# Two attention layers on one core: entry 0's scores in four column strips, the projections of the later entries spread over all of entry 0's pass, and the seams between entries rearranged

## The chip, the core and the metric

The kernel runs on one core of a Trainium2 chip. It is written with a tile framework that places buffers and semaphores; TensorE's instructions run in the order in which the program writes them, those of the other engines in the order that the framework's planner makes from the program order and its own estimates of readiness. The metric is the device time of one execution in microseconds. Engines: PE (TensorE, matrix products; PEld its weight loads), DVE (VectorE), ACT (ScalarE), POOL (GpSimd) and SP (SyncE, which issues most of the DMAs).

## The reference

A batch of 8 entries x[2048, 256] goes through two graph attention layers over the same adjacency matrix adj[2048, 2048], each followed by a residual and a layer norm.

```
layer 0 (8 heads of 32):  x_proj = x W_h;  e_src = x_proj a_src,  e_dst = x_proj a_dst
    e[i,j] = leaky_relu(e_src[i] + e_dst[j], 0.2) + softplus(beta) log(adj[i,j] + 1e-6),  no edge: masked
    h[i]   = sum_j softmax_j(e) x_proj[j]       (per head);   x1 = layernorm(x + h W_out^T)
layer 1:  e = leaky_relu((x1 W1)(x1 W2)^T, 0.2), no edge: masked
    h'[i]  = sum_j softmax_j(e) (x1 W3)[j];     out = layernorm(x1 + relu(h'))
```

## The kernel before

**Layer 0** (class `Gat`, one per entry) never forms the exponent of each pair. The exponent of a leaky ReLU of a sum is the larger of two products, so a tile of 128 keys by 2048 queries is `max(c, r) * mt` in one DVE operation (L336): `c` the query factors of a head, spread over all partitions, `r` a per-key number (`re`), `mt` the mask column, which also holds the adjacency to the power beta. The second per-key factor is multiplied into the value rows `v` beforehand (`scale`, L286). A *unit* is one block of 128 keys for two heads: two L336 tiles, then on PE one product with the values into `val` and one with the per-key factor into `den` (`products`, L361; 16 records each, in four groups of 32 columns). An entry has 64 units: 4 pairs of heads (`hp`) by 16 key blocks (`jt`). For some key blocks (`SUMMED`, L67) DVE or ACT adds the scaled tile to a running sum instead (L343, L349), and PE takes den from the sum at the end. `finish` (L373 to L389) divides: den goes through DRAM and a reciprocal, and one multiply (L389) scales two pairs of heads. There are 4 buffers for score tiles `s`, 2 for `mt`, 3 for `c`.

`output` (L391) applies W_out (L414), adds x, which it loads itself in four pieces `xg` (L400), and takes the layer norm, in four steps. `turn` (L430) transposes x1 (L439) and forms h3 = x1 W3 (L445), in eight steps. **Layer 1** (class `Dot`) has 16 steps of 128 query rows: scores `e` (L475) one step ahead, masked row minimum on DVE (L480), exponent (L481), transposes `pt` (L494) and the product `acc` with h3 (L510).

**The order around the change.** At the start, `scores_first` (L246) computes e_dst and e_src of entry 0 for all 16 row blocks, in 32 products with 128 rows of x as weights and only 16 moving columns; `factors` (L268) then takes their maximum over all rows (one GpSimd reduction) and forms the exponents. In the *first stage* entry 0's 64 units run alone; between them `others()` (L539) computes the projections of the seven other entries, an item for each quarter of an entry: transposes of x (L172), rows (L262), and after the fourth quarter factors, scaling and the store of `v` and `re` to DRAM. The main loop (L575) asks for an item after every second unit, so that the 28 items are done at the 56th unit. Entry 1 comes last, since its values stay in SBUF. The value buffers are two: `v`, and the one that is later h3; the items use them in turns. The first 16 units also build `mt` from the adjacency (L180 to L193).

After that, entry b's layer 0 runs beside entry b-1's layer 1: the loop from L584 mixes `dot.step(fill)`, where `fill(0)`, `fill(1)` and `fill(2)` put units ahead of the step's transposes, before and after `acc`. A *seam* is the stretch in which layer 0 of an entry has ended and its `output` and `turn` are put between the last layer 1 steps of the entry before and the first units of the next one. There `load` (L300) fetches `v` and `re` of the next entry from DRAM. SP issues these loads, the `xg` of `output`, the mask columns, masks and residual rows in one queue: an issue that waits for its buffer holds up those behind it.

Of the kernel before, what the change touches and what calls it, by code (L numbers as in the profile page):

```python
# [9 lines left out]
F32 = mybir.dt.float32  # L10
# [8 lines left out]
P = 128  # L19
# [8 lines left out]
def kernel(  # L28
# [26 lines left out]
    nc = tc.nc  # L55
    B, N, D = x.shape
    H, _, DH = w_proj.shape
    NT = N // P
    KC = D // P
    BK = 512  # L60
    NB = N // BK
    HALF = N // 2
    HP = 2
    NP = H // HP
    IG = BK // P
# [3 lines left out]
    const = ctx.enter_context(tc.tile_pool(name="const", bufs=1))  # L69
# [3 lines left out]
    chunk = ctx.enter_context(tc.tile_pool(name="chunk", bufs=2))  # L73
    small = ctx.enter_context(tc.tile_pool(name="small", bufs=3))
# [3 lines left out]
    def mm_tile(name):  # L78
        return ps.tile([P, BK], F32, tag="mm", name=name)
# [9 lines left out]
    ident = const.tile([P, P], F32)  # L89
# [15 lines left out]
    beta_c = beta[:, 3:4]  # L105


    wp = const.tile([P, KC, D + 2 * H], F32)
    for kc in range(KC):
        nc.sync.dma_start(  # L110
            wp[:, kc, 0:D].rearrange("p (h f) -> p h f", h=H),
            w_proj[:, kc * P:(kc + 1) * P, :].rearrange("h p f -> p h f"),
        )
    for a, dst in ((a_dst, wp[:, :, D:D + H]), (a_src, wp[:, :, D + H:])):
        a_bc = small.tile([P, D], F32, tag="row", name="a_bc", bufs=4)
        nc.sync.dma_start(a_bc, bass.AP(tensor=a.tensor, offset=a.offset, ap=[[0, P], [1, D]]))
        for kc in range(KC):
            wa = small.tile([P, D], F32, tag="row", name="wa", bufs=4)
            nc.vector.tensor_mul(wa, wp[:, kc, 0:D], a_bc)
            nc.vector.tensor_reduce(dst[:, kc, :], wa.rearrange("p (h f) -> p h f", h=H), AX.X, ALU.add)  # L120
# [36 lines left out]
    v_d = dram.tile([B, P, NT, D], F32, name="v_d")  # L157
    re_d = dram.tile([B, P, 2, NT, H], F32, name="re_d")
# [73 lines left out]
    class Gat:  # L232
# [12 lines left out]

        def scores_first(self, xt):  # L246

            t = mm_tile("both")
            for it in range(NT):
                for kc in range(KC):  # L250
                    nc.tensor.matmul(t[:, ts(it, 2 * H)], xt[:, kc, ts(it, P)], wp[:, kc, D:],
                                     start=(kc == 0), stop=(kc == KC - 1))
            nc.scalar.copy(self.both.rearrange("p t h -> p (t h)"), t[:, 0:NT * 2 * H])

        def rows(self, g, xt, scores=True):

# [11 lines left out]
        def factors(self):  # L268

            top = small.tile([P, 2, H], F32, name="top", bufs=1)  # L270
            ed, es = self.both[:, :, 0:H], self.both[:, :, H:2 * H]
            nc.vector.tensor_reduce(top[:, 0, :], ed.rearrange("p t h -> p h t"), AX.X, ALU.max)
            nc.gpsimd.partition_all_reduce(top[:, 1, :], top[:, 0, :], P, bass_isa.ReduceOp.max)
            self.sums_c = small.tile([P, H, NT], F32, name="cs", bufs=1)
            nc.vector.tensor_tensor(self.sums_c, es.rearrange("p t h -> p h t"),
                                    top[:, 1, :].unsqueeze(2).to_broadcast([P, H, NT]), ALU.add)
            nc.vector.tensor_tensor(ed, ed, top[:, 1:2, :].to_broadcast([P, NT, H]), ALU.subtract)
            self.re = small.tile([P, 2, NT, H], F32, name="re", bufs=2)
            nc.scalar.activation(self.re[:, 0], ed, AF.Exp, scale=-(1.0 - ALPHA))
            nc.scalar.activation(self.re[:, 1], ed, AF.Exp)  # L280

# [17 lines left out]

        def load(self):  # L300
            self.v = whole.tile([P, NT, D], F32, name="v")
            nc.sync.dma_start(self.v, v_d[self.b])
            self.re = small.tile([P, 2, NT, H], F32, name="re", bufs=2)
            nc.sync.dma_start(self.re, re_d[self.b])

        def query_rows(self, h):

# [83 lines left out]
        def output(self):  # L391


            b = self.b
            xb = x[b].rearrange("(t p) d -> p t d", p=P)
            xs = []

            def load(g):
                xs.append(chunk.tile([P, IG, D], F32, tag="ht", name="xg", bufs=3))
                nc.sync.dma_start(xs[g], xb[:, ts(g, IG), :])  # L400

            for g in range(NB - 1):
                load(g)
            for g in range(NB):
                if g == 1:
                    load(NB - 1)
                st = small.tile([P, IG, nc.vector.BN_STATS_DIM], F32, name="st4", bufs=1)
                mv = small.tile([P, IG, nc.vector.BN_AGGR_DIM], F32, name="mv4", bufs=2)
                z = self.ht[:, ts(g, IG)].rearrange("p t k i -> p t (k i)")
                for k in range(0, IG, 2):  # L410
                    y = mm_tile("y").rearrange("p (t c) -> p t c", t=2)
                    for i in range(2):
                        for kc in range(KC):
                            nc.tensor.matmul(y[:, i, :], self.ht[:, g * IG + k + i, kc, :], wot[:, kc, :],  # L414
                                             start=(kc == 0), stop=(kc == KC - 1))
                    nc.vector.tensor_add(z[:, k:k + 2, :], y, xs[g][:, k:k + 2, :])
                    for i in range(k, k + 2):
                        nc.vector.bn_stats(st[:, i, :], z[:, i, :])
                        nc.vector.bn_aggr(mv[:, i, :], st[:, i, :])
                f = small.tile([P, 2, IG], F32, name="f4", bufs=2)  # L420
                nc.scalar.activation(f[:, 0, :], mv[:, :, 1], AF.Ln, bias=eps_ln)
                nc.scalar.activation(f[:, 0, :], f[:, 0, :], AF.Exp, scale=-0.5)
                nc.vector.scalar_tensor_tensor(f[:, 1, :], mv[:, :, 0], -1.0, f[:, 0, :], ALU.mult, ALU.mult)
                for k in range(IG):
                    nc.scalar.activation(z[:, k, :], z[:, k, :], AF.Identity, bias=f[:, 1, k:k + 1],
                                         scale=f[:, 0, k:k + 1])
                nc.scalar.dma_start(x1_d[b].rearrange("(t p) d -> p t d", p=P)[:, ts(g, IG), :], z)
                yield
# [94 lines left out]
    gats = [Gat(b) for b in range(B)]  # L523
# [15 lines left out]
    def others():  # L539


        items = [(gat, g) for gat in gats[2:] + gats[1:2] for g in range(NB)]
        xgs, xts = [], []

        def load(n):
            if n < len(items):
                xgs.append(load_x(items[n][0].b, items[n][1]))

        def turn(n):
            if n < len(items):  # L550
                xts.append(chunk.tile([P, KC, BK], F32, tag="ht", name="xt", bufs=3))
                transpose_x(xgs[n], xts[n])
                load(n + 1)

        load(0)
        turn(0)
        for n, (gat, g) in enumerate(items):
            turn(n + 1)
            if g == 0:
                gat.begin(("v", "h3")[n // NB % 2])  # L560
            gat.rows(g, xts[n])
            if g == 0 and n > 0:
                items[n - 1][0].queries()
            if g == NB - 1:
                gat.factors()
                for k in range(NB):
                    gat.scale(k)
                if gat.b > 1:
                    gat.store()
            yield  # L570
        gats[1].queries()
        yield

    pieces = [others(), later_weights()]
    for k in range(NP * NT):  # L575
        g0.step()
        if k % 2 == 1:
            next(pieces[0], None)
            if k > NT and k % 4 == 1:
                next(pieces[1], None)  # L580


    dot = None
    for b in range(1, B + 1):  # L584
        gat, fresh = gats[b - 1], gats[b] if b < B else None

        def layer_0(count):
            if fresh:
                fresh.step(count)

        if b > 1 and fresh:
            fresh.load()
        rows = gat.output()

        def output(count):
            for _ in range(count):
                next(rows)

        if dot is None:
            layer_0(3)  # L600
            output(4)
            layer_0(1)
        else:

            dot.step(lambda k: layer_0((0, 0, 2)[k]))
            dot.step(lambda k: (output((1, 1, 2)[k]), layer_0((0, 1, 1)[k])))
        for _ in gat.turn():
            layer_0(1)
        dot = Dot(gat)
        dot.step(lambda k: layer_0((2, 1, 1)[k]))  # L610
        for i in range(NT - 3):
            dot.step(lambda k: layer_0((0, 2 - (i % 3 == 2), 2)[k]))
    dot.step()
# [32 lines left out]
```

## Time and profile before

4389.39 us, median of 3 runs (4389.17 to 4393.52). The profiled execution spans 4389.8 us.

| engine | busy us | share | what most of it is |
|---|---|---|---|
| PE | 4243.0 | 97% | val and den products (L361), acc (L510), e (L475) |
| DVE | 3624.5 | 83% | score tiles (L336: 2353.5), sums (L343: 632.2) |
| ACT | 1666.5 | 38% | exponents and copies out of PSUM |
| POOL | 6.4 | 0% | eight reductions of the factors |

The DMA engines are busy 54.6% of the span. Busy PE is modelled from pipelined records, so it is an upper limit. The page divides the span into forty slices of 110 us and gives busy shares in tenths; the table by stage gives the same for any stretch. Entry 0's layer 0 ends at about 488 us; from then on an entry takes about 508.5 us (from one load of `v` to the next), and the last stage, from about 4050 us, is layer 1 of the last entry alone.

### The profile page before, as it was taken

The numbers are of one execution on the slowest core, as the hardware profiler recorded it, in microseconds if no ns is written. First come the engines' busy times: TensorE is split into PE (matmuls) and PEld (weight loads), VectorE is DVE, ScalarE is ACT, GpSimd is POOL, SyncE is SP. The second block draws the span as 40 slices with busy tenths as digits, with TensorE's granted clock in tenths as the row PEclk, the third lists the DMA queues.
The fourth block names the chain that finished last, engine by engine and source line by source line (L and its number), as shares of the span: only waits on it lengthen the run. The fifth ranks groups of instructions, "written<-read, shape, count | busy, mean of one in ns | idle before, by whom it ended". The sixth has DMA issues, their size and how long they took to land.

```text
span 4389.8 us, 59761 instructions
## 1 busy us (share of the span) xinstructions
PE 4243.0 (97%) x25052; PEld 2226.0 (51%) x25052; DVE 3624.5 (83%) x2597; ACT 1666.5 (38%) x3020; POOL 6.4 (0%) x14
## 2 busy tenths in 40 slices
PE   7899899999999999999999999999999999999999
PEld 5454344445444545445445454445555454545666
DVE  6888888998989898997989988898889889898222
ACT  6622233333333323333333334333333333333454
POOL 0000000000000000000000000000000000000000
PEclk9999999999999999999999999999999999999999
DMA  7887666656555554556555555556545565554111
GB/s 234 292 302 273 209 221 211 230 193 225 191 189 189 197 197 168 195 192 213 180 193 185 188 196 185 192 187 216 184 166 199 184 214 184 191 183 147 60 50 41
DMA packets 250958, 839.10 MB, mean 191 GB/s; under 512 B 32320, under 2 KB 150848, under 8 KB 175424
## 3 DMA queue, kind: packets, MB, share of 16 engines
q1 hardware_dynamic: 215360, 801.71, 52.1%
q10 hardware_dynamic: 35328, 33.56, 2.2%
q8 instruction: 196, 3.21, 0.3%
q14 instruction: 74, 0.61, 0.0%
HBM read 761.53 MB, written 73.14 MB: 190 GB/s over the span
## 4 chain that ended last, share of the span: by engine, by line
PE 56%; DVE 18%; issue 9%; DMA 4%; ACT 2%; SPq 1%; ACTq 0%; DVEq 0%
PE acc L510 15%; PE e L475 14%; DVE s L336 11%; PE val L361 11%; PE den L361 7%; DVE d L343 4%; PE pt L494 4%; DMA mt<-mt_d 3%; PE y L414 2%; PE h1p L465 2%; PE h3p L445 1%; DVE p L480 1%; ACT p L481 1%; DMA rc<-dn 1%; SPq L379 0%
## 5 line engine op out<-in xcount | busy, mean ns | idle before, releaser
L336 DVE SCALAR_TENSOR_TENSOR s<-c,re,mt 128x2048 f32<-128x2048 f32 x1024 | 2353.5, 2342 | 194.4 <-PE den L361 132.8
L361 PE MATMUL val<-s,v 128*32 128x512 f32 x8192 | 1030.0, 604 | 67.8 <-DVE s L336 67.3
L510 PE MATMUL acc<-h,pts 128*128 128x256 f32 x4096 | 949.9, 380 | 2.2 <-ACT pts L496 1.4
L475 PE MATMUL e<-x1t,h 128*128 128x512 f32 x2048 | 906.0, 595 | 6.8 <-ACT h L467 6.8
L510 PEld LDWEIGHTS acc<-h,pts 128*128 128x128 f32 x4096 | 748.1, 190 | 92.8 <-ACT pts L496 6.9
L361 PE MATMUL den<-s,re 128*32 128x512 f32 x5568 | 709.0, 599 | 3.3 <-ACT dn L376 3.3
L343 DVE SCALAR_TENSOR_TENSOR d<-s,re,d 128x2048 f32<-128x2048 f32 x272 | 632.2, 2344 | 0.0
L475 PEld LDWEIGHTS e<-x1t,h 128*128 128x128 f32 x2048 | 379.1, 190 | 459.5 <-issue 416.5
L496 ACT COPY pts<-pt 128x512 f32<-128x512 f32 x512 | 298.2, 583 | 766.4 <-PE pt L494 759.5
L361 PEld LDWEIGHTS val<-s,v 128*32 128x32 f32 x8192 | 244.3, 110 | 676.4 <-issue 516.3
L477 ACT ACTIVATE p<-e 128x512 f32<-128x512 f32 x512 | 303.1, 596 | 433.6 <-PE e L475 429.9
L480 DVE CUSTOM_DVE_ANT_0 p<-p,pen 128x2048 f32<-128x2048 f32 x128 | 292.9, 2288 | 198.2 <-ACT p L477 197.5
L361 PEld LDWEIGHTS den<-s,re 128*32 128x32 f32 x5568 | 194.3, 111 | 429.6 <-issue 417.0
L494 PEld LDWEIGHTS pt<-ident,p 128*128 128x128 f32 x2048 | 239.0, 141 | 223.2 <-issue 163.0
L481 ACT ACTIVATE p<-p,neg 128x2048 f32<-128x2048 f32 x128 | 256.7, 2006 | 242.4 <-DVE neg L480 242.4
L494 PE MATMUL pt<-ident,p 128*128 128x128 f32 x2048 | 319.3, 279 | 6.5 <-ACT p L481 6.5
L517 ACT ACTIVATE z<-acc,rec 128x256 f32<-128x256 f32 x128 | 60.9, 475 | 370.4 <-PE acc L510 340.0
L518 DVE TENSOR_TENSOR z<-z,x1r 128x256 f32<-128x256 f32 x128 | 53.8, 421 | 156.1 <-ACT z L517 155.9
L445 PE MATMUL h3p<-w3s,x1t 128*128 128x256 f32 x512 | 122.6, 383 | 15.4 <-ACT x1t L440 14.5
L414 PE MATMUL y<-wot,ht 128*128 128x256 f32 x512 | 120.5, 393 | 9.8 <-DVE ht L389 9.8
L262 PE MATMUL proj<-wp,xt 128*128 128x272 f32 (+1 forms) x512 | 125.5, 398 | 0.1
L349 ACT ACTIVATE d<-s,re 128x2048 f32<-128x2048 f32 x56 | 112.1, 2005 | 29.1 <-DMA mt<-mt_d 23.5
(85 smaller groups left out, 1877.3 us busy)
## 6 DMA issues: line engine op xcount, KB each, us to landing
mt<-mt_d SPq DMA_DIRECT2D x496, 1024.0 KB, 4.9
c<-c_d SPq DMA_DIRECT2D x64, 1024.0 KB, 7.1
pen<-pen_d SPq DMA_DIRECT2D x112, 512.0 KB, 3.4
xg<-in_x_dram SPq DMA_DIRECT2D x60, 512.0 KB, 6.0
adj_t<-in_adj_dram SPq DMA_DIRECT2D x16, 1024.0 KB, 7.9
mt_d<-mt SPq DMA_DIRECT2D x16, 1024.0 KB, 5.7
rb<-rec_d SPq DMA_DIRECT2D x64, 256.0 KB, 4.6
x_d<-ht ACTq DMA_DIRECT2D x32, 512.0 KB, 3.6
```

The source lines that it names most:

```text
L336: nc.vector.scalar_tensor_tensor(sa, self.cs[a], self.re[:, 0, jt, h:h + 1], mt, ALU.max, ALU.mult)
L343: nc.vector.scalar_tensor_tensor(d, sa, e[:, jt - 1, h:h + 1], d, ALU.mult, ALU.add)
L361: nc.tensor.matmul(dst[ts(q, DH), ts(c, BK)], weights[q % 2], s[q % 2][:, ds(q // 2 * HALF + c * BK, BK)], start=start, stop=stop)
L414: nc.tensor.matmul(y[:, i, :], self.ht[:, g * IG + k + i, kc, :], wot[:, kc, :], start=(kc == 0), stop=(kc == KC - 1))
L445: nc.tensor.matmul(t[:, ts(i, D)], x1t[:, kc, ts(2 * (j - 1) + i, P)], w3s[:, kc, :], start=(kc == 0), stop=(kc == KC - 1))
L475: nc.tensor.matmul(t, self.h1[:, kc, ts(it % IG, P)], self.x1t[:, kc, ts(c, BK)], start=(kc == 0), stop=(kc == KC - 1))
L477: nc.scalar.activation(p[:, ts(c, BK)], t, AF.Prelu, alpha=ALPHA)
L480: nc.vector.tensor_tensor_reduce(p, p, pen, -1.0, FMAX, ALU.add, ALU.min, neg)
L481: nc.scalar.activation(p, p, AF.Exp, bias=neg, scale=-1.0, accum_out=den)
L494: nc.tensor.transpose(t[:, ts(k, P)], p[:, ts(g * IG + k, P)], ident)
L496: nc.scalar.copy(pt, t)
L510: nc.tensor.matmul(acc, now[:, ts(k, P)], self.h3[:, j, :], start=(j == 0), stop=(j == NT - 1))
```

## The change

Five edits go together. (1) Entry 0's scores: the 32 columns a_dst, a_src and 16 zero columns become the weights, x moves, and four strips of 512 rows fill the four column groups of the array; a copy, four transposes and a copy with rearrangement bring them to the old layout. (2) Projections: 27 items are spread evenly over the 64 units, and the last one follows the first three units of entry 1. (3) Entry 1 comes fifth in the order of projections and keeps the `v` buffer from then on, so that the last two entries both use the h3 buffer; `re` gets a third buffer. (4) GpSimd issues the loads of `v`, `re` and `xg`. (5) At seams, units come two at a time, after every second step of `turn`, and none stands between the second output step and `acc`. They aim at a shorter start, at less waiting when the projections have run out and at seams, and at fewer changes between 32-column and full-width products.

```diff
-    wp = const.tile([P, KC, D + 2 * H], F32)
+    wp = const.tile([P, KC, D + DH], F32)
+    nc.vector.memset(wp[:, :, D + 2 * H:], 0.0)
...
         def scores_first(self, xt):
-            t = mm_tile("both")
-            for it in range(NT):
-                for kc in range(KC):
-                    nc.tensor.matmul(t[:, ts(it, 2 * H)], xt[:, kc, ts(it, P)], wp[:, kc, D:],
+            t = mm_tile("scores")
+            for kc in range(KC):
+                for q in range(NB):
+                    nc.tensor.matmul(t[ts(q, DH), :], wp[:, kc, D:], xt[:, kc, ts(q, BK)],
                                      start=(kc == 0), stop=(kc == KC - 1))
-            nc.scalar.copy(self.both.rearrange("p t h -> p (t h)"), t[:, 0:NT * 2 * H])
+            s = chunk.tile([P, BK], F32, tag="pt", name="scores", bufs=2)
+            nc.scalar.copy(s, t)
+            t = mm_tile("scores_t")
+            for k in range(IG):
+                nc.tensor.transpose(t[:, ts(k, P)], s[:, ts(k, P)], ident)
+            nc.scalar.copy(self.both.rearrange("p (q k) h -> p k q h", k=IG),
+                           t.rearrange("p (k q h) -> p k q h", k=IG, h=DH)[:, :, :, 0:2 * H])
...
-            self.re = small.tile([P, 2, NT, H], F32, name="re", bufs=2)
+            self.re = small.tile([P, 2, NT, H], F32, name="re", bufs=3)
...
-            nc.sync.dma_start(self.v, v_d[self.b])
+            nc.gpsimd.dma_start(self.v, v_d[self.b])
-            nc.sync.dma_start(self.re, re_d[self.b])
+            nc.gpsimd.dma_start(self.re, re_d[self.b])
...
-                nc.sync.dma_start(xs[g], xb[:, ts(g, IG), :])
+                nc.gpsimd.dma_start(xs[g], xb[:, ts(g, IG), :])
...
-        items = [(gat, g) for gat in gats[2:] + gats[1:2] for g in range(NB)]
+        order = gats[2:-2] + gats[1:2] + gats[-2:]
+        items = [(gat, g) for gat in order for g in range(NB)]
...
-                gat.begin(("v", "h3")[n // NB % 2])
+                gat.begin("h3" if n // NB % 2 or gat is order[-1] else "v")
...
-        gats[1].queries()
+        order[-1].queries()
...
-    pieces = [others(), later_weights()]
+    projections, weights = others(), later_weights()
+    due = (B - 1) * NB - 1
     for k in range(NP * NT):
         g0.step()
-        if k % 2 == 1:
-            next(pieces[0], None)
-            if k > NT and k % 4 == 1:
-                next(pieces[1], None)
+        if (k + 1) * due // (NP * NT) > k * due // (NP * NT):
+            next(projections)
+            if k > NT:
+                next(weights, None)
...
             layer_0(3)
+            for _ in projections:
+                pass
             output(4)
             layer_0(1)
         else:
             dot.step(lambda k: layer_0((0, 0, 2)[k]))
-            dot.step(lambda k: (output((1, 1, 2)[k]), layer_0((0, 1, 1)[k])))
-        for _ in gat.turn():
-            layer_0(1)
+            dot.step(lambda k: (output((1, 1, 2)[k]), layer_0((0, 0, 2)[k])))
+        for k, _ in enumerate(gat.turn()):
+            if k % 2 == 1:
+                layer_0(2)
         dot = Dot(gat)
-        dot.step(lambda k: layer_0((2, 1, 1)[k]))
+        dot.step(lambda k: layer_0((2, 0, 2)[k]))
```

More of the change, by code (lines that the diff above doesn't have):

```diff
@@ L113 @@
         )
-    for a, dst in ((a_dst, wp[:, :, D:D + H]), (a_src, wp[:, :, D + H:])):
+    for a, dst in ((a_dst, wp[:, :, D:D + H]), (a_src, wp[:, :, D + H:D + 2 * H])):
         a_bc = small.tile([P, D], F32, tag="row", name="a_bc", bufs=4)
@@ L301, in load @@
             self.v = whole.tile([P, NT, D], F32, name="v")
-            nc.sync.dma_start(self.v, v_d[self.b])
-            self.re = small.tile([P, 2, NT, H], F32, name="re", bufs=2)
-            nc.sync.dma_start(self.re, re_d[self.b])
+            nc.gpsimd.dma_start(self.v, v_d[self.b])
+            self.re = small.tile([P, 2, NT, H], F32, name="re", bufs=3)
+            nc.gpsimd.dma_start(self.re, re_d[self.b])
         def query_rows(self, h):
```

## Prediction

> **What bounds the kernel now.** I read the busy shares first, then the forty slices, then the work by stage, and last the order of work on single engines around one seam.
>
> ```profile
> PE 4243.0 (97%) x25052; PEld 2226.0 (51%) x25052; DVE 3624.5 (83%) x2597; ACT 1666.5 (38%) x3020; POOL 6.4 (0%) x14
> ...
> PE   7899899999999999999999999999999999999999
> ```
>
> TensorE (PE) is the bound nearly everywhere, with DVE close behind. A change can gain only where PE stands idle or does needless work. The table by stage finds such places (columns: stretch, length, busy PE, PEld, DVE, ACT, POOL, granted PE clock, DMA share, GB/s).
>
> ```profile
> 460.00:480.00 20.00, 17.00 (x128) 4.41 (x128) 17.93 (x9) 0.00 (x0) 0.00 (x0) 0.83 0.55 193
> 480.00:500.00 20.00, 15.20 (x114) 3.63 (x110) 15.03 (x8) 5.03 (x4) 0.00 (x0) 0.94 0.63 228
> 500.00:520.00 20.00, 10.34 (x45) 4.23 (x43) 17.11 (x8) 2.00 (x1) 0.00 (x0) 0.76 0.75 254
> ...
> 1525.00:1550.00 25.00, 20.87 (x110) 11.82 (x103) 20.25 (x29) 7.30 (x16) 0.00 (x0) 0.86 0.72 273
> ```
>
> The last projection ends at 454.7; from there to the first seam PE waits for DVE. The fourth line is the seam between entries 1 and 2 (numbered from 0). Its PE order, with the wait before a row in brackets:
>
> ```profile
> 1527.02 3.72 PE L414 MATMUL y<-wot,ht 128*128 128x256 f32 x16
> 1530.57 0.60 PE L494 MATMUL pt<-ident,p 128*128 128x128 f32 x4
> 1531.01 3.62 PE L414 MATMUL y<-wot,ht 128*128 128x256 f32 x16
> 1536.16 1.04 PE L361 MATMUL val<-s,v 128*32 128x512 f32 x2 [1.53 <-DVE s L336]
> 1539.80 2.78 PE L361 MATMUL val<-s,v 128*32 128x512 f32 x11 [2.60 <-DVE s L336]
> ...
> 1542.38 3.77 PE L361 MATMUL den<-s,re 128*32 128x512 f32 x15
> ```
>
> PE waits 4.1 us for one unit's score tiles, and then runs at half speed (a den product is 1.90 us elsewhere). Why DVE was late stands in SyncE's queue (start, issue time) and on DVE:
>
> ```profile
> 1517.70 0.94 SPq L199 DMA_DIRECT2D mt<-mt_d  x1
> 1531.49 0.37 SPq L400 DMA_DIRECT2D xg<-in_x_dram  x1
> 1531.90 0.51 SPq L199 DMA_DIRECT2D mt<-mt_d  x1
> ```
> ```profile
> 1529.05 0.69 DVE L416 TENSOR_TENSOR ht<-y,xg 128x512 f32<-128x512 f32 x1 [5.60 <-PE y L414]
> ```
>
> The fourth x load needs a buffer that an output step frees; SyncE stood at it for 14 us and the next mask column `mt` stood behind it. Meanwhile DVE idled 5.6 us. All five later seams look alike: in each, PE's waits come to 6.2 us on L336 and 2.7 us on the x1t copy.
>
> [...] what it buys here is that the wait stands on another sequencer [...], as the 14 us above agree. [...] DVE's seam work is mostly two-tensor operations of 2.3 us per 2048; no row of before shows a GpSimd DMA. [...] a 128*32 product takes 1.74 us start to start before another one, 1.83 to 1.85 before a 128*128 transpose. [...]
>
> **The change, part by part.**
> *Entry 0's scores (L246).* Before: 64 records in 10.2 us (15.7 to 25.9) and a copy. The new form has the shape of one val product (16 records, 4 column groups): 1.9, then a copy 0.6, four transposes 0.6, a copy 0.4, handovers about 0.4: 3.9 against 10.6. Those 6.7 us are on the path: ACT waited 9.4 us for these scores, with the first mask's Ln (ready at 19.5, run at 28.1) queued behind. The adjacency loads allow it. I take **-6** (0 to -8). The memset of 16 columns hides in DVE's first waits.
>
> *Projections to the end.* A unit costs PE 3.5 us (202.2, 205.6, 209.2) and DVE two tiles of 2.27 = 4.55; a projection item costs PE 4.6 (transposes 0.9, rows 3.7). In the first 16 units, which build the masks and where DVE is 19.1 of 20 us busy, 8 items become floor(16*27/64) = 6 and two entries' scalings (4 x 1.22 plus about 1) become one: DVE loses 6 us, which is only partly on the path, so **-4** (0 to -8). The other 48 units ran from 202.2 to 487.6, 285 us. PE work before 454.7 was 42 x 3.5 + 20 x 4.6 + 5 (query transposes, weights) = 244 in 252.5 us, so 3.5% over. Now 48 x 3.5 + 21 x 4.6 + 5 = 270, times 1.035 = 279. DVE has 48 x 4.55 + 5 x 6 + 5 = 253, so PE stays the bound: **-6** (+3 to -12).
>
> *First seam.* From the last product (487.6) to the end of y (532.6) took 45 us. y waited for the multiply L389, 29 us in, which stood behind score tiles delayed by `mt` and den. The chain itself is about 19 us (copies 3.0, rc 2.4 + 2.6, reciprocal 0.4, rec 3.1, rb 0.8 + 4.6, multiply 2.3). The new PE work beside it is five products (8.7) and the last item (4.6), so that item is hidden. With some of its scalings ahead of the multiply I put y at 23 instead of 29: **-6** (+3 to -10).
>
> *Entry 1 fifth, the last two entries both in h3.* New wait: the last entry's value copies (ACT, behind them PE's PSUM tiles) need the store of the one before. In the trace, the last copy of an entry was at 350.9, the store issued at 358.2, and such a store lands in 8.2: 366.4. The next entry's first copy would come three units and a transpose later, at about 363. Three PSUM tiles soften it: **+2** (0 to +8). `re` with three buffers costs nothing; it keeps entry 1's factors aside.
>
> *Seams, x and v on GpSimd, units by pairs (6 seams, entries 1 to 6).* At the seam shown the new PE order after 1527.0 is y, pt, y (to 1534.6), then acc with three pt (8.3), y (7.0, to 1549.9). Before, this ended at 1561.4 with one 3.6 us unit in it: the 4.1 us of waits and 3.8 us of half speed are gone, as the waiting unit moved behind y and `mt` is no longer behind x. Units 2 and 3 add 5.3: turn starts at 1555.2 instead of 1563.2. In turn, DVE needs 8 x 4.55 + 3 x 4.6 = 50 us from 1553.4, PE 42 us, so DVE bounds it and ends near 1604; before, its last product ended at 1611.8. So the h3p wait and the later waits come back as waits for DVE, and the gain is what the start gives: **-8 per seam** (-3 to -12), **-48**. GpSimd's transfers: [...] SyncE's took 8.7 and 6.0. I take SyncE's. v is issued at 1502.7 and first used after 1523, x used from 1529: hidden at both prices. If `re` queued behind v, it would land near 1508 and delay the first score tiles by up to 7 us, to about 1517 for the fourth, still ahead of 1523. Pairing saves four pairs of mode changes in turn, 0.8 us, not counted where DVE is the bound; at entry 0's seam, **-1**.
>
> Sum: -6 -4 -6 -6 +2 -48 -1 = -69: 4389.4 - 69 = **4320**.
>
> **Rivals.** *A, the seams give half back*: DVE is 83% busy overall and nearly full in turn; pairs ask for four tiles at once with four s buffers. Then -3 or -4 a seam and -15 in the first stage: 4389 - 21 - 15 = **4353**. For it: the 50 us against 42. Against: DVE starts those units 8 us earlier. *B, waits vanish altogether*: PE also keeps its clock in turn; 13 us a seam (all that the waits, the slow clock and mode changes come to) and -35 in the first stage: 4389 - 78 - 35 = **4276**. Against: the same DVE sum. *C, slower*: GpSimd's issue is late (one queue for v, re, x; the factor reduction too), x holds up y by 4 us a seam, and the h3 store and the late last item eat what the first stage gains: 4389 + 24 = **4413**. For it: no GpSimd DMA is in the trace, and y and turn need x and the h3 buffer soon. Against: 20 us of slack for v, and GpSimd busy 6.4 us in all.
>
> **How the numbers follow.** Forecast 0.62, A 0.18, B 0.10, C 0.10. The sum of my costs' far ends would be about -130 to +5; taking them as independent leaves -35 to -105. So 4285 to 4356, which holds the forecast's spread and most of A and leaves out C and B. Slower by over 0.2% is C less its mild part: 0.08; within 0.2%: 0.03; faster: 0.89.
>
> **What would show it.** The first score tile on DVE at about 35 instead of 41.0; no stretch after 455 where PE is under 9 of 10 busy until the finish of entry 0; unit-to-unit distance 5.6 us there. At later seams: no wait on L336 between the second y and acc, no half-speed den, `mt` issued every 5 us while x waits on GpSimd, and entry to entry (v load to v load) about 500.5 instead of 508.5 us. I would be wrong if DVE's tiles follow late in turn, if L264's copies stand long on the h3 store, or if L416 waits on x.

## The result, and the profile after

The changed kernel takes **4406.89 us** (median of 4, 4404.5 to 4409.58) against 4390.5 us of the kernel before on the same chip: a ratio of **1.0037** [1.0019, 1.0054] (the brackets give a 95% interval, here and below). The forecast was 4320 (4285 to 4356). The profiled execution spans 4403.5 us, 13.7 more than before. From the page:

```profile
PE 4243.3 (96%) x25008; PEld 2224.6 (51%) x25008; DVE 3621.2 (82%) x2598; ACT 1668.0 (38%) x3021; POOL 37.2 (1%) x58
...
PE   7889899999999999999999999999999999999899
```

The sums of PE, DVE and ACT are those of before within 0.1%, and two slices of PE have turned from 9 to 8, the third and the 38th. Only landmarks in time show where the span moved: the copies out of `val` that follow each sixteen units mark the end of the 16th unit (the first) and of entry 0 (the fourth), and the loads of `v` mark the entries.

| stretch | before, us | after, us | change | foretold |
|---|---|---|---|---|
| start and first 16 units | 195.6 | 186.6 | -9.0 | -10 |
| entry 0's other 48 units | 292.0 | 312.8 | **+20.8** | -6 + 2 |
| from there to the first load of v | 506.1 | 510.1 | +4.0 | -6 -1 |
| five entries, v to v | 5 x 508.74 | 5 x 507.94 | **-4.0** | -40 |
| last load of v to the end | 852.4 | 854.2 | +1.8 | -8 |

**Entry 0.** The table by stage, before and then after, for stretches in the middle and at the end of entry 0 (length, busy PE, PEld, DVE, ACT, POOL, granted PE clock, DMA share, GB/s):

```profile
205.00:225.00 20.00, 18.81 (x140) 8.62 (x133) 20.00 (x15) 4.42 (x15) 0.62 (x1) 1.00 0.85 313
225.00:245.00 20.00, 20.00 (x150) 10.02 (x153) 14.05 (x7) 5.41 (x21) 0.00 (x0) 1.00 0.96 361
```
```profile
205.00:225.00 20.00, 17.93 (x148) 7.46 (x140) 15.95 (x12) 3.37 (x12) 0.37 (x1) 1.00 0.62 226
225.00:245.00 20.00, 17.60 (x121) 7.55 (x125) 14.71 (x8) 3.68 (x13) 0.00 (x0) 0.91 0.82 299
460.00:480.00 20.00, 15.73 (x103) 5.21 (x96) 16.63 (x13) 2.03 (x6) 0.36 (x1) 0.83 0.63 234
480.00:500.00 20.00, 20.00 (x155) 9.27 (x157) 13.68 (x7) 4.96 (x18) 0.00 (x0) 1.00 0.73 271
```

The hole after 455 is filled in part: from 480 to 500 PE is now full, but from 460 to 480 it is busy for 15.73 us against 17.00, at the same slow clock (0.83). Holes have come up earlier, and in them **neither** engine is fully busy, PE or DVE. The order on PE around one shows why, with DVE's beneath:

```profile
215.85 1.92 PE L369 MATMUL val<-s,v 128*32 128x512 f32 x16
...
219.31 1.90 PE L369 MATMUL val<-s,v 128*32 128x512 f32 x16
...
225.98 1.04 PE L369 MATMUL val<-s,v 128*32 128x512 f32 x2 [3.05 <-DVE s L344]
228.24 2.78 PE L369 MATMUL val<-s,v 128*32 128x512 f32 x11 [1.22 <-DVE s L344]
```
```profile
210.12 6.87 DVE L344 SCALAR_TENSOR_TENSOR s<-c,re,mt 128x2048 f32<-128x2048 f32 x3
216.91 0.36 DVE L280 TENSOR_REDUCE top<-both 128x8 f32<-128x128 f32 x1
...
219.03 4.63 DVE L294 TENSOR_TENSOR v<-v,re 128x1024 f32<-128x1024 f32 x4 [0.64 <-ACT re L288]
223.58 9.12 DVE L344 SCALAR_TENSOR_TENSOR s<-c,re,mt 128x2048 f32<-128x2048 f32 x4
...
242.62 9.14 DVE L344 SCALAR_TENSOR_TENSOR s<-c,re,mt 128x2048 f32<-128x2048 f32 x4 [4.63 <-PE den L369]
```

Three units follow one another from 215.85. DVE meanwhile works on an item's factors and scaling for 6.7 us (216.91 to 223.58); the third unit finds no score tile, waits 3.05 us and then runs at about half speed (11 records in 2.78 us, where the unit before it takes 1.92 us for 16; granted clock 0.76 from 225 to 232 us). At 242.62 it is DVE that stands 4.63 us, because all four score buffers are full.

Three of the five long waits of PE in these 48 units are of this kind (226, 352 and 469 us). The other two, the longest, stand behind a load. DVE stood for an `mt` and for a `c`, and PE behind it:

```profile
180.99 0.38 SPq L166 DMA_DIRECT2D xg<-in_x_dram  x1
182.02 0.86 SPq L200 DMA_DIRECT2D mt<-mt_d  x2
190.12 6.88 DVE L344 SCALAR_TENSOR_TENSOR s<-c,re,mt 128x2048 f32<-128x2048 f32 x3 [8.96 <-DMA mt<-mt_d]
192.62 1.89 PE L369 MATMUL val<-s,v 128*32 128x512 f32 x2 [4.42 <-DVE s L344]
...
294.40 0.38 SPq L317 DMA_DIRECT2D c<-c_d  x1
300.57 2.35 DVE L344 SCALAR_TENSOR_TENSOR s<-c,re,mt 128x2048 f32<-128x2048 f32 x1 [6.15 <-DMA c<-c_d]
302.98 2.78 PE L369 MATMUL val<-s,v 128*32 128x512 f32 x11 [4.53 <-DVE s L344]
```

The `mt` was issued right behind an x load of the projections that SyncE had stood at. The `c` was issued as its buffer came free; DVE, late from a scaling, had no finished tiles in hand to cover the load. In all, PE waited 26.4 us for tiles in these 48 units (11.7 before), with a granted clock of 0.96 (0.99 before), and DVE 42.6 us for buffers (25.3 before).

**The seam.** It is 14.3 us later than in the kernel before. PE's order after, then SyncE's issues before and after, GpSimd's, and DVE's reciprocal before and DVE after:

```profile
1532.17 1.89 PE L518 MATMUL acc<-h,pts 128*128 128x256 f32 x8
...
1537.10 2.43 PE L518 MATMUL acc<-h,pts 128*128 128x256 f32 x8 [3.04 <-ACT pts L504]
1539.46 3.12 PE L369 MATMUL val<-s,v 128*32 128x512 f32 x16
...
1548.97 4.85 PE L422 MATMUL y<-wot,ht 128*128 128x256 f32 x14 [2.33 <-DVE ht L397]
```
```profile
1497.31 0.32 SPq L309 DMA_DIRECT2D c<-c_d  x1
...
1502.74 0.32 SPq L302 DMA_DIRECT2D v<-v_d  x1
1507.25 2.41 SPq L379 DMA_DIRECT2D rc<-dn  x4
...
1533.40 0.75 SPq L309 DMA_DIRECT2D c<-c_d  x1
```
```profile
1511.29 0.32 SPq L317 DMA_DIRECT2D c<-c_d  x1
...
1514.40 0.42 SPq L317 DMA_DIRECT2D c<-c_d  x1
1520.15 0.32 SPq L395 DMA_DIRECT2D rb<-rec_d  x1
1521.23 2.41 SPq L387 DMA_DIRECT2D rc<-dn  x4
```
```profile
1517.00 0.55 POOL L310 DMA_DIRECT2D v<-v_d  x1 [473.27 <-PE val L369]
1517.54 0.75 POOL L408 DMA_DIRECT2D xg<-in_x_dram  x1
```
```profile
1513.01 0.35 DVE L380 RECIPROCAL rc<-rc 128x32 f32<-128x32 f32 x1 [1.70 <-DMA rc<-dn]
```
```profile
1531.94 0.35 DVE L388 RECIPROCAL rc<-rc 128x32 f32<-128x32 f32 x1 [7.80 <-DMA rc<-dn]
1532.21 2.23 DVE L488 CUSTOM_DVE_ANT_0 p<-p,pen 128x2048 f32<-128x2048 f32 x1
```

The foretold waits on score tiles in front of y are gone. New ones stand in their place: 3.04 us in `acc`, 2.33 us in y, and behind them 3.3 us of half speed (granted clock 0.51 from 1539 to 1542 us; val 3.12 us in place of 1.92, the y record 4.85 in place of 14/16 of 3.72, acc 2.43 in place of 1.89). They come from DVE, which stands 7.80 us at the **reciprocal** (1.70 us before) with layer 1's mask step L488 behind it. `rc` is four loads of 4 KB; from issue to reciprocal they take 10.5 us (mean of six seams; 5.5 before). Two things differ in the queues: `v`, `xg` and `re` go from GpSimd at once, and SyncE, which used to stand at `v`, has sent a **second c** (1 MB) and an rb ahead of `rc`; before, the second c came 26 us behind it.

### The profile page after: what moved, and what is told of

Its sections match the earlier page's. It is cut to its first block, busy times and chain, and to the rows that moved or that the text cites. A ratio compares the mean times of both kernels' runs of the same rounds, so it can differ in the third digit from the quotient of the medians.

```text
span 4403.5 us, 59803 instructions
## 1 busy us (share of the span) xinstructions
PE 4243.3 (96%) x25008; PEld 2224.6 (51%) x25008; DVE 3621.2 (82%) x2598; ACT 1668.0 (38%) x3021; POOL 37.2 (1%) x58
## 5 line engine op out<-in xcount | busy, mean ns | idle before, releaser
L488 DVE CUSTOM_DVE_ANT_0 p<-p,pen 128x2048 f32<-128x2048 f32 x128 | 292.6, 2286 | 193.3 <-ACT p L485 192.8
L489 ACT ACTIVATE p<-p,neg 128x2048 f32<-128x2048 f32 x128 | 256.7, 2005 | 246.3 <-DVE neg L488 246.3
```

The source lines that it names most:

```text
L488: nc.vector.tensor_tensor_reduce(p, p, pen, -1.0, FMAX, ALU.add, ALU.min, neg)
L489: nc.scalar.activation(p, p, AF.Exp, bias=neg, scale=-1.0, accum_out=den)
```

## The experiments

"Entry to entry" is the mean of five distances between loads of `v`. The theory after the result: the pace (how the items are spread over the units) costs the first stage, and `v` off SyncE's queue costs the seams.

### Which of the moved loads costs the seams

All three loads back, only x back, only v and re back:

```diff
-nc.gpsimd.dma_start(self.v, v_d[self.b])
+nc.sync.dma_start(self.v, v_d[self.b])
-nc.gpsimd.dma_start(self.re, re_d[self.b])
+nc.sync.dma_start(self.re, re_d[self.b])
-nc.gpsimd.dma_start(xs[g], xb[:, ts(g, IG), :])
+nc.sync.dma_start(xs[g], xb[:, ts(g, IG), :])
```

> The changed kernel with v, re and x at seams issued by SyncE again; all else as changed. Theory L (the loads by GpSimd go out earlier and move more slowly, so that the den round trip of the seam, 8.4 us for rc instead of 4.4, holds DVE's queue and PE): rc lands in about 4 us again, no wait of acc on the pts copy, and an entry takes about 500 us instead of 507.9, so the whole is near 4365. Rival Q (x queued ahead of mt was the seam's cost, as the prediction had it, and pairs alone do not help): an entry takes 508 us or more, the whole stays at or above 4403. Rival D (DVE's own sum bounds the seam whatever the loads do): 507 to 508, about 4403.

4372.8 us, 0.9953 [0.9937, 0.9970]; entry to entry 503.1.

> The changed kernel with only the x loads of the output step issued by SyncE again; v and re stay on GpSimd. If the early x load beside v is what slows the den round trip, rc lands in 4 to 5 us and an entry takes about 501 us (whole near 4367). If v from GpSimd is itself the slow part (12.4 us against 8.7), rc still takes 7 to 8 us and an entry stays within 2 us of 507.9 (whole near 4400).

4384.25 us, 0.9982 [0.9975, 0.9989]; entry to entry 504.9, and `rc` still takes 9.9 us.

> The changed kernel with v and re issued by SyncE again; only x stays on GpSimd. The mirror of the run before: if v from GpSimd is the slow part, an entry takes about 501 us (whole near 4367); if the early x load is, it stays near 507 (whole near 4400). If both are needed for the collision, both mirrors gain.

**4367.99 us**, 0.9946 [0.9931, 0.9961]; entry to entry 502.3, `rc` 5.4 us. So `v` with the small re (128 KB; the two were not moved apart) is the costly move; x on GpSimd does no harm by itself.

### The first stage: pace, scaling or buffers

The pace, the order of entries and the kept buffers as before:

```diff
-        if (k + 1) * due // (NP * NT) > k * due // (NP * NT):
-            next(projections)
-            if k > NT:
+        if k % 2 == 1:
+            next(projections, None)
+            if k > NT and k % 4 == 1:
...
-        order = gats[2:-2] + gats[1:2] + gats[-2:]
+        order = gats[2:] + gats[1:2]
...
-                gat.begin("h3" if n // NB % 2 or gat is order[-1] else "v")
+                gat.begin(("v", "h3")[n // NB % 2])
```

> The changed kernel with the projections as before: an item after every second unit, entry 1 last, value buffers in turns. Theory P (three units in a row after an entry's last item outrun the two units of score tiles that fit in the buffers, while DVE scales the values for 6.7 us): the four waits of 4.3 us with their half-speed matmuls go, and the first load of v comes at 985 to 988 instead of 1009.5 (start still 9 us earlier than before); the whole near 4381. Rival M (the first stage is bound by the sums of PE and DVE work, and spreading is neutral; the loss is in the first seam): first load of v at 1003 or later, whole near 4398.

4383.83 us, 0.998 [0.9973, 0.9988]; the 48 units take 289.9 us, the first `v` is loaded at 988.1. The loss of the first stage is in these edits.

The new pace, with the scaling split in two and put behind the next entry's first and second item (for the last two entries it stays in one piece):

```diff
+            if later and g < 2:
+                for k in (2 * g, 2 * g + 1):
+                    later[0].scale(k)
...
-                for k in range(NB):
-                    gat.scale(k)
+                    later.append(gat)
```

> The changed kernel, but the four scalings of an entry's values follow the next entry's first two items, two after each, and the store after the last of them (for the last two entries they stay where they were). The same instructions in all. Theory P in its full form (6.7 us of scaling in one piece, met by three units in a row): three of the four waits of 4.3 us and their half-speed matmuls go, about 8 us each, so the first load of v comes at 985 to 992 instead of 1009.5, and the whole is near 4385. Rival (three units in a row outrun the buffers by themselves): first load of v at 1003 or later, whole near 4400.

4394.89 us, 1.0007 [0.9999, 1.0016]; the 48 units still take 308.8 us. PE's waits in them (total, times, longest), of the changed kernel and of this one:

```profile
PE val L369 <- DVE s L344: 26.4, 16, 4.5
```
```profile
PE val L369 <- DVE s L344: 23.0, 14, 4.8
```

The burst alone is not it. Where it is split, the wait of 3.05 us falls to 0.78 us (those at 226 and 352 us in the changed kernel); where it is not, it stays (3.06 us at 462). But the two waits behind loads stay too (4.33 and 4.77 us), and smaller ones come up elsewhere.

The old pace alone, with v and re on SyncE, but with the new order and both last entries in h3 (the first hunk of the first diff of this section):

> The changed kernel with v and re on SyncE again and the pace of the projections of before (one after every second unit); entry 1 fifth and the last two entries both kept in h3 stay as changed. Theory (the pace alone costs the 21 us of units 16 to 63: three units in a row outrun DVE): those 48 units take about 290 us as in the kernel before, the first v load comes near 988, entry to entry 502.4, median about 4345. Rival (the order and the store into h3 cost part of it): about 295 to 312 us for the 48 units, first v load at 994 to 1010, median 4351 to 4368.

4352.25 us, 0.9913 [0.9897, 0.9930]; 298.9 us for the 48 units. That is 6.6 to 9 us above the old pace and order together (289.9 above, 292.3 in the next section); 5.5 of them are one wait, for a copy by ScalarE into h3 that itself waits for the store of the values before out of it:

```profile
PE val L369 <- DVE s L344: 10.4, 9, 3.6
PE proj L270 <- ACT both L274: 5.5, 1, 5.5
```

In the changed kernel that wait is absent. So undoing the **pace** alone takes 13.9 of the 20.8 us away, and the waits behind loads go with it; undoing pace and order takes away all of it (20.5 and 22.9 us in two runs). What is left at the old pace, 6.6 to 9 us, comes with the order. The new pace with the old order was not run.

### The parts put together

The old pace, order and buffers, and v and re on SyncE; the score strips, the pairs and x on GpSimd stay:

> Scores in strips and units by pairs as changed, x on GpSimd; projections paced and ordered as before, v and re on SyncE. If the two causes found so far add up (first load of v at 988, an entry 502.3, the rest 845.9), the span is 988 + 5 x 502.3 + 845.9 = 4345 and the time about 4347. If the first stage and the seams depend on each other, it stays above 4355.

**4344.45 us**, 0.9892 [0.9877, 0.9906], span 4345.3, 292.3 us for the 48 units: the causes add up. In the stretch of the prediction's table (this seam starts 3.9 us earlier than that of before) PE is busy at full clock:

```profile
1525.00:1550.00 25.00, 24.33 (x137) 19.08 (x139) 22.98 (x48) 10.74 (x27) 0.75 (x1) 1.00 0.58 202
```

With v and re on SyncE, the units one at a time and in the places of before:

```diff
...
-        for k, _ in enumerate(gat.turn()):
-            if k % 2 == 1:
-                layer_0(2)
+        for _ in gat.turn():
+            layer_0(1)
...
```

> As the changed kernel with v and re on SyncE and x on GpSimd (4368), but the units at seams one at a time and at their places of before. If the pairs and the moved unit bring the gain of the seams, an entry takes 507 us or more again (whole near 4398). If freeing the mt loads from the x wait brings it, as the prediction's reading of SyncE's queue said, an entry stays near 503 (whole near 4372).

4370.55 us, 0.9952 [0.9937, 0.9967], entry to entry 502.0 against 502.3: the pairs bring nothing once x is out of SyncE's queue.

The kernel before with the score strips and x on GpSimd alone (the first hunks of the change and one line):

> The kernel before with two parts of the change alone: entry 0's scores in four strips, and x loaded by GpSimd. Theory (these two are the whole gain: 5 us at the start and in the first units, 6 us a seam because mt no longer stands behind x): first score tile at 36.4, first v load at about 988, entry to entry about 502.3, median about 4345, as in the run with old pace, order and v on SyncE. Rival (the units moved and paired at the seams are needed with it): entry to entry 504 to 507, median 4355 to 4375.

4347.71 us, 0.9903 [0.9888, 0.9918], entry to entry 502.3: within the intervals, these two parts are the whole gain.

### Why v outside SyncE's queue costs

v in four loads by GpSimd:

```diff
-nc.gpsimd.dma_start(self.v, v_d[self.b])
+for g in range(NB):
+    nc.gpsimd.dma_start(self.v[:, ts(g, IG), :], v_d[self.b][:, ts(g, IG), :])
```

> The changed kernel with v loaded by GpSimd in four pieces of 4 KB per partition instead of one of 16 KB. If the long packets of v hold up the small rc transfers behind them, rc lands in 4 to 5 us and an entry takes 503 to 505 (whole near 4386). If what matters is only that v comes from GpSimd, an entry stays within 1.5 us of 507.9 (whole near 4405).

4394.58 us, 1.0009 [1.0002, 1.0015]; entry to entry 506.0, `rc` 9.5 us: 1.9 us an entry better than the changed kernel, which neither forecast had, and a third of what v on SyncE gives.

The changed kernel with `nc.scalar` in place of `nc.gpsimd` for v:

> The changed kernel with v loaded by ScalarE in place of GpSimd; re and x stay with GpSimd. Nothing is left out. Theory (it is that v is off SyncE's queue, not that GpSimd issues it): SyncE again sends a second c ahead of rc, rc's wait is 6 to 8 us, entry to entry 506 to 509, median about 4400 (more if ScalarE's other work is held up behind v). Rival (transfers issued by GpSimd are slow by themselves): rc's wait 2 to 3 us, entry to entry 502 to 503, median about 4370.

4415.44 us, 1.005 [1.0035, 1.0065]; entry to entry 509.3, `rc` 12.6 us. **GpSimd is not the cause.** In this version the planner put L488 ahead of the reciprocal, so the mask step isn't held up; y's multiply L397 is, and PE waited 6.86 us for it at the seam behind entry 1.

rc's four loads by ScalarE, `nc.scalar.dma_start(rc[...` for `nc.sync` at L387:

> The changed kernel with rc's four small loads issued by ScalarE, so that c and rb no longer stand ahead of them in the same queue. Nothing is left out. Theory (rc waits its turn behind c and rb in SyncE's queue): rc lands in 3 to 4 us at the seams, entry to entry about 503, median about 4375. Rival (the 16 engines are shared, and rc is slow whatever queue it is in while v, c, x and re are under way): the reciprocal's wait stays 5 to 8 us, entry to entry 506 to 508, median 4390 to 4407.

4412.63 us, 1.0042 [1.0025, 1.0059]; entry to entry 508.2, `rc` 10.5 us, as in the changed kernel. A queue without c and rb in it did not help `rc`. (The first `v` comes 10 us later in this run.)

The second c by GpSimd:

```diff
-nc.sync.dma_start(c, c_d[self.b, h:h + 1, :].to_broadcast([P, N]))
+queue = nc.gpsimd if self.b > 0 and h == 1 else nc.sync
+queue.dma_start(c, c_d[self.b, h:h + 1, :].to_broadcast([P, N]))
```

> The changed kernel, except that the second c of every entry from 1 on (1 MB, the one that SyncE otherwise issues just ahead of rc) is loaded by GpSimd, whose queue has v in front of it. Nothing is left out. Theory (the crowd in SyncE's queue: rc lands late because a further 1 MB stands before it): rc's wait at the reciprocal falls from 7.8 us to about 2, entry to entry about 503, median about 4370 to 4380. Rival (v on GpSimd's queue shares the engines with rc and slows it by itself, whatever SyncE sends): rc's wait stays 6 to 8 us, entry to entry 506 to 508, median 4393 to 4407.

4422.69 us, 1.0067 [1.0052, 1.0082]; entry to entry 511.3, `rc` 12.5 us. The planner put this c ahead of v (1512.1 against 1517.5), so it did not test what it was made for; SyncE still sent another c and an `mt` of 1 MB each ahead of `rc`.

A slice of v on SyncE, the rest on GpSimd:

```diff
-nc.gpsimd.dma_start(self.v, v_d[self.b])
+nc.sync.dma_start(self.v[:, 0:1, :], v_d[self.b][:, 0:1, :])
+nc.gpsimd.dma_start(self.v[:, 1:, :], v_d[self.b][:, 1:, :])
```

> The changed kernel, except that SyncE loads the first of sixteen slices of v, so that it stands at v's buffer as in the kernel before, and GpSimd loads the other fifteen and re. Nothing is left out. Theory (the crowd: without v's wait on its queue SyncE sends another 1 MB c load and an rb load into the seam, and rc's small transfers land behind them): no second c issue before v, rc lands in about 4 us, the reciprocal's wait is 2 us or less, entry to entry about 502.5 us, median about 4369. Rival (v from GpSimd is slow by itself, or its transfers push rc aside): rc stays at about 8 us, entry to entry 506 to 508, median 4390 to 4407.

4430.39 us, 1.0092 [1.0077, 1.0107]; entry to entry 511.5, `rc` 13.5 us. Outside both: the second c came 0.9 us behind the slice, even closer to `rc`. It separates nothing.

1 MB more beside `rc`, in the version with v and re on SyncE:

```diff
+            if lo > 0 and b > 0:
+                for q in range(2):
+                    nc.gpsimd.dma_start(spare_d[q], dn)
```

> The version with v and re on SyncE and x on GpSimd (4367.99 us, entry to entry 502.28, rc's wait 2.6 us at the seam), with 1 MB more in the seam: at the end of every entry's second and fourth pair of heads GpSimd also stores dn twice (0.5 MB each) into a spare buffer in DRAM, just as rc is loaded. Nothing is left out. Theory (it is the bytes under way in the 16 engines that push rc back, in whatever queue): 1 MB at the 400 GB/s of this stretch is 2.6 us, so rc's wait at the seam goes to about 5 us, entry to entry to 504 to 505, median 4378 to 4386. Rival (it is v outside SyncE's queue that does it, not the bytes): wait 2 to 3 us, entry to entry 502.3, median 4368.

4369.22 us, 0.9955 [0.9939, 0.9972]. `rc` goes from 5.4 to 7.5 us (2.1 us for the MB), as the theory had it, but entry to entry stays at 502.4, as the rival had it. DVE in the version put together above shows what takes it up:

```profile
1507.99 0.35 DVE L388 RECIPROCAL rc<-rc 128x32 f32<-128x32 f32 x1 [1.79 <-DMA rc<-dn]
1510.29 2.29 DVE L488 CUSTOM_DVE_ANT_0 p<-p,pen 128x2048 f32<-128x2048 f32 x1 [1.94 <-ACT p L485]
```

With `rc` in time, L488 waits 1.94 us more for ScalarE; so about the first 2 us of rc's lateness are free. In the changed kernel, and in the run with 1 MB more, L488 follows the reciprocal at once.

The second c cut to 64 KB in the changed kernel (head 1 of entries 1 to 7 then reads 128 columns sixteen times over):

```diff
-nc.sync.dma_start(c, c_d[self.b, h:h + 1, :].to_broadcast([P, N]))
+n = P if self.b > 0 and h == 1 else N
+nc.sync.dma_start(c[:, 0:n], c_d[self.b, h:h + 1, 0:n].to_broadcast([P, n]))
```

> The changed kernel with the second c of every entry from 1 on cut from 1 MB to 64 KB: only its first 128 columns are loaded, and head 1's scores read them sixteen times over, so head 1 of these entries is left wrong; v, re and x stay on GpSimd. Theory (the bytes under way): 1 MB less is 2.6 us, rc's wait falls from 7.8 us to about 5 and entry to entry to 505 to 506, median about 4390. Rival (v outside SyncE's queue shares the engines with rc's small packets and slows them whatever else is sent): wait 7 to 8 us, entry to entry 508, median 4400 to 4407. If head 1's score tiles take longer on DVE in this form, that is to be set off.

4411.62 us, 1.0053 [1.0038, 1.0068]; entry to entry 509.6, `rc` 11.4 us. Against the theory at first sight; but SyncE sent an `mt` of 1 MB ahead of `rc` (1513.72, 2.65 us after v), and as much was moved as in the changed kernel. The run doesn't decide between the two.

v in two halves, SyncE's and GpSimd's, with x and re on SyncE; and the same with a quarter and three quarters:

```diff
-nc.gpsimd.dma_start(self.v, v_d[self.b])
+nc.sync.dma_start(self.v[:, 0:8, :], v_d[self.b][:, 0:8, :])
+nc.gpsimd.dma_start(self.v[:, 8:, :], v_d[self.b][:, 8:, :])
```

> The changed kernel with x, re and the first half of v on SyncE and the second half of v on GpSimd. Nothing is left out. SyncE now stands at v's buffer with 1 MB of its own, and in its order the second c comes only behind rc; ahead of rc are v, an rb and an x1r more than with all of v on SyncE, about 0.4 MB. Theory (bytes under way): about 4.4 MB from 3 us before v to the reciprocal, rc at the reciprocal 6 to 6.5 us after its issue, entry to entry about 503, median about 4373. Rival (v's bytes in a second queue beside SyncE's slow rc down by themselves): rc 8 us or more after its issue, entry to entry over 504.5, median over 4380.

4367.58 us, 0.995 [0.9935, 0.9965]; entry to entry 502.3, `rc` 7.1 us.

> As the run with half of v on each queue, but SyncE loads only the first quarter of v and GpSimd three quarters. Nothing is left out. The one other difference is in SyncE's order: the second c (1 MB) now goes ahead of rc, and the rb behind it. Theory (bytes under way): about 5.2 MB, rc at the reciprocal 8 to 9 us after its issue, entry to entry 503.5 to 505, median 4376 to 4384; so 2 us or so of rc's time go with that c. Rival: rc as late as in the run with halves, or later only by what a larger share on GpSimd costs.

4398.9 us, 1.002 [1.0013, 1.0028]; entry to entry 507.4, `rc` 9.6 us. SyncE's issues with halves, and then with a quarter:

```profile
1519.68 0.32 SPq L310 DMA_DIRECT2D v<-v_d  x1
...
1524.18 2.44 SPq L388 DMA_DIRECT2D rc<-dn  x4
...
1538.82 0.32 SPq L318 DMA_DIRECT2D c<-c_d  x1
```
```profile
1519.57 0.32 SPq L310 DMA_DIRECT2D v<-v_d  x1
...
1520.47 0.43 SPq L318 DMA_DIRECT2D c<-c_d  x1
1524.07 2.42 SPq L388 DMA_DIRECT2D rc<-dn  x4
```

Here `v` is on two queues both times, and the visible difference is the **second c ahead of rc**; the time differs by 31 us, where 3 to 11 were expected. GpSimd's share of v differs too, but with all of v on GpSimd and x on SyncE an entry took 504.9 us, less than with three quarters. An entry loses 5.1 us where `rc` comes 2.5 us later. PE's waits between 1500 and 2005 us, here with a quarter, show where; with halves these two are 0.8 and 0.5 us:

```profile
PE h3p L454 <- ACT x1t L449: 3.2, 1, 3.2
PE acc L519 <- ACT pts L505: 2.5, 2, 2.0
```

The wait in `acc` is that behind the reciprocal, as in the changed kernel. The one in `turn` (h3p) grows as much and was not followed back to `rc`; in the changed kernel it is 0.2 us a seam. The bytes moved from 3 us before the load of `v` to the reciprocal, at the seam behind entry 1:

| version | MB | rc to reciprocal, us | entry to entry, us |
|---|---|---|---|
| v on SyncE, x on GpSimd | 4.0 | 5.4 | 502.3 |
| halves | 4.6 | 7.1 | 502.3 |
| v on SyncE, 1 MB more | 5.1 | 7.5 | 502.4 |
| quarter | 5.3 | 9.6 | 507.4 |
| x on SyncE, v on GpSimd | 5.7 | 9.9 | 504.9 |
| v in four loads | 5.9 | 9.5 | 506.0 |
| rc on ScalarE | 6.1 | 10.5 | 508.2 |
| changed kernel | 6.2 | 10.5 | 507.9 |
| c cut to 64 KB | 6.4 | 11.4 | 509.6 |
| a slice of v on SyncE | 6.8 | 13.5 | 511.5 |
| second c on GpSimd | 7.0 | 12.5 | 511.3 |
| v on ScalarE | 7.1 | 12.6 | 509.3 |

A longer stretch holds more bytes at a given rate, so the column alone proves no cause. The added MB shows that more bytes make `rc` later, and the pair of halves and quarter that a c ahead of it goes with a dearer entry. In these runs `rc` up to 7.5 us costs nothing, and from 9.5 us on an entry costs 3 to 9 us more; but the cost does not follow `rc` alone (504.9 us at 9.9, 507.4 at 9.6).

## Why the prediction was wrong

- **Scores and first 16 units, -10**: right, -9.0; the first score tile is at 36.40 us, 35 was foretold.
- **The other 48 units, -6 (+3 to -12)**: this step failed, +20.8. It summed PE's and DVE's work and took the larger ("PE stays the bound"). DVE's sum was right (253 foretold, 250.9 measured). But sums hold only if buffers smooth them out. Four score tiles are two units; the even spread of 27 items over 64 units makes runs of three. PE then outruns DVE in a run, DVE stands still in the item behind it, and at two places DVE had no lead to cover a load of `mt` or `c`: PE's waits for tiles rose from 11.7 to 26.4 us, and its busy time, at the slower clock behind them, from 279.7 to 285.8. By experiment the pace alone makes 13.9 of the 20.8 us, pace and order all of it; that runs of three do it, and not the place of an item beside a load, is read from the trace. More score buffers were not tried.
- **h3 store, +2 (0 to +8)**: no wait in the changed kernel, 5.5 us at the old pace.
- **First seam, -6 - 1**: from the end of entry 0 to the end of y 47.7 us against 44.9, so +2.8. About 5 us of it are the 27th item, which PE runs behind entry 0's last product (501.0 to 506.0) and which the prediction counted in the 48 units; counted there, those lost 26 us and this seam gained 2. The 28th item was called hidden, and it was not: PE waited 4.89 us for its factors, that is for the end of a multiply on DVE, the reduction on GpSimd (2.31 us) and DVE's step behind it:

```profile
521.92 3.93 PE L270 MATMUL proj<-wp,xt 128*128 128x272 f32 x16
530.75 0.45 PE L303 MATMUL est<-ident,cs 128*128 128x128 f32 x1 [4.89 <-DVE cs L283]
```

- **Later seams, -8 each**: the reading of SyncE's queue, that `mt` stood behind x, was right, and with x alone moved it gives -6.4 an entry (mis-sized by 1.6). In the changed kernel 0.8 is left. The step that failed is "v ... hidden at both prices". It asked when `v` lands and is used, which holds (it lands 12.4 us after its issue, 8.7 before, and no product waits for it); not **what SyncE does when it no longer stands at v**. It sends a second c and an rb; x and re follow v on GpSimd. `rc`, which has a price in the first seam's sum but none in these, is loaded while 2.2 MB more move than with `v` on SyncE (6.2 against 4.0, in a stretch that is 5 us longer; the 1 MB added by itself cost it 2.1 us), and comes 5 us later.
- **Pairing**: no gain in turn, as foretold; none elsewhere either (502.0 against 502.3).
- **Rivals**: the time lies near C's 4413, but C's reasons fail. GpSimd's issue was not late (0.55 us for v, at 1517.00; with ScalarE `rc` takes 12.6 us against 10.5), no wait of y's addition for x is in the trace, and the h3 store cost nothing. Its late last item is right: PE's 4.89 us above. That the time is near C's is luck.

The prediction took it that a load given to another issuer could do no harm. That was the author's assumption. It holds for x alone (502.3 us an entry) and fails for `v`: `rc` takes 10.5 us with `v` from GpSimd and 12.6 with `v` from ScalarE, against 5.4 with `v` from SyncE; SyncE's freed time is what let the second c go ahead. Nor do the small loads come sooner from another queue: 10.5 us on ScalarE's and on SyncE's. Why was not found.

## What to carry to other kernels

In the kernel before, a load that waited for its buffer also held back what stood behind it in its queue: SyncE issued nothing from 1518.64 to 1531.49 us, where it stood at an x load, and the next `mt` went out at 1531.90. Before such a load is moved to another issuer, look up what the old queue will send in its place, and which small transfer on the path is loaded beside it (here 1 MB more took `rc` from 5.4 to 7.5 us). A rate worked out from sums of work per engine needs a second question: does the longest run of one kind of work fit into the buffers between the engines, and does the slower engine keep a lead that covers its next load?

## What the runs showed of the hardware

In the changed kernel's seam, from 1514 to 1526 us, with `v`, c, mt and x under way, the 16 engines move 351 to 456 GB/s (in steps of 3 us), at a busy share of 0.96 to 1.09. Four loads of 4 KB take 4.6 us (a seam of the kernel before) to 14.4 us (one with a slice of v on SyncE) from issue to reciprocal, and in the mean 10.5 us in SyncE's queue (changed kernel) as in ScalarE's. 1 MB more cost them 2.1 us (7.5 against 5.4). The issue of a 2 MB load took 0.32 us on SyncE and 0.55 us on GpSimd. After waits of 3.0 to 4.5 us PE ran at about half speed: 11 records in 2.78 us (at 302.98), where 16 take 1.92; the granted clock from 302 to 306 us was 0.61.
